# A four-layer cross-attention kernel: layer 0's head outputs joined into dense tiles, steps for the other batch moved, PSUM banks reassigned

## The chip, the cores and the metric

The kernel runs on one core of a Trainium2 chip, in one launch. The metric is the device time of one execution in microseconds (us), here the median of a few runs. The profile is one execution recorded by the hardware profiler; it has a time of its own.

## The reference

Four layers, each `x = x + attention(layernorm(x), ctx)` and then `x = x + ffn(layernorm(x))`, in fp32, with x of 4 x 256 x 256 (batch, token, width) and ctx of 4 x 512 x 128. Layer 0's attention has 16 heads of 16 columns; the last 16 context rows ("dca") have keys and values of their own, a softmax of their own, and their result is added:

```python
q = _ln((x @ Wq + bq).reshape(b, s1, H, HD), qn_w, qn_b)
...
ctx = _attn(qT, k.transpose(0, 2, 1, 3), v.transpose(0, 2, 1, 3))
...
ctx = ctx + DCA_WEIGHT * ctx_dca
return ctx @ Wo + bo
```

Layers 1 to 3 have 16 heads of 128 with 8 key and value heads, all on the same ctx. The feed-forward parts differ: F0 picks the 4 strongest of 64 small "arrows" for each token; F1 is a mixture of 8 experts, 2 for each token, plus a shared MLP; F2 picks one of two MLPs for each token; F3 sends 64 tokens of each batch through an MLP and scales the others.

## The kernel before

x stays in SBUF (`x_sb[b]`) for the whole launch. The order of the work on PE (TensorE), ACT (ScalarE), DVE (VectorE) and POOL (GpSimd) is written out by hand (`manual_schedule`): the order of the calls in the program is the order in each engine's queue, and each engine takes its queue in that order. DMAs are mostly issued by SP. The stages follow one another on the trace as layer 0's attention (0 to about 165 us), F0 with the first folding (to 244), attention 1 (to 576), F1 with the second folding (to 702), attention 2 (to 1035), F2 with the third (to 1092), attention 3 (to 1422), F3.

**PSUM.** `bank()` (L850) gives out the 8 banks. In layer 0 and F0 the tag "o" has 2 banks and all others share a ring of 6. Later "s" has 4, "mm" 2, "t" 1 and "o" 1. A step that asks for a bank waits until its last reader is done.

**Layer 0's attention** loops over 4 batches and 4 groups of 4 heads, in two halves, so 8 steps i for a batch. A step computes `scores` (L1314, with the exponential on ACT), the `values` (L1327) of the group before, after every second step its `quotient` (L1348), and beside these, in `ahead` and `between` (L1503, L1514), the next batch's Norm, projections, head norms (`Scale`, whose product writes `pad` on DVE, L1231) and transposes of `pad` (L1296), and the batch before's `output0` (L1362). Each head's values tile has 32 columns: 16 of ones, which yield the softmax divisor, and 16 of values. The output of `values` (po) thus holds divisors and results on alternate runs of 16 partitions. `quotient` transposes po in 32x32 blocks on DVE (L1354), takes the reciprocal (L1356), transposes that back in a broadcast (L1357), multiplies (L1359), and adds main and dca results on POOL into `oT` (L1360). `oT` therefore has four tiles of 128 partitions of which half are useless, and `wo0` is loaded (L1069) in four tiles likewise, so `output0` takes four matmuls for each chunk of 128 tokens (L1366), then adds the bias on DVE (y_sb, L1374) and to x on POOL (L1375). `project_v` (L1185) fills the values, three ACT copies for each batch.

**F0** runs `Arrows(n)` for the 8 token chunks: `vectors` (matmul paf), `routes` (selection on DVE, last product twof on POOL, L1427), `turned` (transposes puTf, L1435) and `output` (pyf, L1448).

**Folding** (L974) multiplies, for each layer 1 to 3, query by key weights (pm, L985; to m_sb on ACT, L993) and value by output weights (pn, L1001; to n_sb on DVE, L1004), one pair of heads after the other, both in tag "mm".

**Attention 1 to 3** (L1689) loops over b and 8 head pairs hp: scores ps (L1817), exponential on ACT (L1820), po (L1825), half sums of the probabilities on POOL and DVE (L1836 to L1850), the divisors of four pairs (pz, L1857; rz, L1866), and the division (L1871, L1872). `beside1` and `beside3` (L2117, L3051) put steps of the next feed-forward part for batch b-1 beside given head pairs: in layer 1 Norm, its tokens, `turned1` (transposes and a store, L2058) and `chosen` (the choice of experts, L2067); in layer 3 the Router's steps (L2878).

**F1** has `Shared` (L2146), and 23 `Block`s (L2290) of 128 gathered tokens: `weights` (the expert's index read into registers of PE and DVE, and its weights copied, L2312, L2317), `turn_in` (transposes pxg, L2306, to ACT), `rise` (pgu, L2325) and `fall` (pyr, L2341; yr on ACT, L2348). F2's `Block2` (L2592) is alike for 7 blocks.

```python
if b > 0 and i in (4, 5):
    output0(b - 1, (i - 4,))
```

## Time and profile before

| | us |
|---|---|
| median of 3 runs | 1453.56 |
| the runs | 1453.41, 1453.56, 1455.87 |
| the profiled execution | 1455.58 |
| its span, first to last instruction | 1453.9 |
| PE busy in it | 1421.4 |
| mean granted clock of PE | 0.994 of full speed |

The span is the profiled execution without the 1.7 us around it. A row of the profile names a line of the kernel, an engine, an operation, its output and inputs; "idle before" is the time in which that engine stood, and the name behind the arrow is the instruction whose end released it. "f32 128x256" is 128 partitions of 256 elements. A matmul in fp32 appears as two records. PEclk is the clock granted to PE, as a share of full speed.

### The profile page before, as it was taken

How to read it: one execution, taken by the hardware profiler on the slowest of the kernel's cores; microseconds unless marked ns; L12 is line 12 of the kernel's file. 1: busy time of each engine (PE TensorE's matmuls, PEld its weight loads, DVE VectorE, ACT ScalarE, POOL GpSimd, SP SyncE). 2: the span in 40 equal slices, each digit the busy share in tenths (PEclk: the TensorE clock that was granted, in tenths of full speed). 3: DMA queues.
4: the chain of work that ended last, by engine and by line, in shares of the span. 5: the costliest groups of instructions: out<-in, count | busy, mean ns of one | idle time of the engine just before them, and what ended most of it. 6: DMA issues, size and time to landing. Idle time of an engine off the chain costs nothing.

```text
span 1453.9 us, 20222 instructions
## 1 busy us (share of the span) xinstructions
PE 1421.4 (98%) x7421; PEld 937.0 (64%) x7421; DVE 914.0 (63%) x2004; ACT 585.9 (40%) x1124; POOL 677.1 (47%) x796
## 2 busy tenths in 40 slices
PE   9999999999999999999999999999999999999998
PEld 7665676566556666777556666655875566666656
DVE  6666773666676556543576666548755766767675
ACT  4666343433433332244543333333454433333331
POOL 2222232576655454131366665665314765456560
PEclk9999999999999999999999999999999999999999
DMA  5000220310000001164020000000331000000000
GB/s 167 2 2 2 73 72 1 79 32 0 8 1 8 1 8 32 39 203 103 30 72 2 23 1 1 8 0 8 95 124 44 19 1 1 0 1 0 0 1 32
DMA packets 49591, 47.06 MB, mean 32 GB/s; under 512 B 8169, under 2 KB 45386, under 8 KB 49484
## 3 DMA queue, kind: packets, MB, share of 16 engines
q1 hardware_dynamic: 45884, 37.56, 8.6%
q0 software_dynamic: 2496, 6.82, 1.8%
q8 instruction: 61, 1.00, 0.3%
q10 hardware_dynamic: 1104, 1.31, 0.3%
q14 instruction: 46, 0.38, 0.1%
HBM read 38.86 MB, written 6.82 MB: 31 GB/s over the span
## 4 chain that ended last, share of the span: by engine, by line
PE 88%; DVE 7%; POOL 2%; issue 1%; ACT 1%; DVEq 0%; ACTq 0%; POOLq 0%
PE ps L1817 22%; PE po L1825 21%; PE paq L1787 5%; PE pao L1787 4%; PE pbq L1787 4%; PE pbo L1787 4%; PE pgu L2325 2%; PE ps L1321 2%; PE pyf L1448 2%; PE po L1331 2%; PE paf L1398 1%; PE py L1907 1%; PE pm L985 1%; PE psh L2161 1%; PE pn L1001 1%
## 5 line engine op out<-in xcount | busy, mean ns | idle before, releaser
L1836 POOL TENSOR_TENSOR half<-pT 128x1024 f32<-128x1024 f32 x93 | 218.8, 2353 | 322.6 <-ACT pT L1820 255.2
L1817 PE MATMUL ps<-qT,cT 128*128 128x512 f32 x768 | 345.5, 592 | 0.0
L1825 PE MATMUL po<-pT,c_sb 128*128 128x512 f32 x768 | 345.3, 592 | 0.0
L1820 ACT ACTIVATE pT<-ps,mbias 128x512 f32<-128x512 f32 x384 | 263.7, 687 | 155.5 <-PE ps L1817 143.9
L1825 PEld LDWEIGHTS po<-pT,c_sb 128*128 128x128 f32 x768 | 145.8, 190 | 183.2 <-issue 183.2
L1817 PEld LDWEIGHTS ps<-qT,cT 128*128 128x128 f32 x768 | 138.9, 190 | 138.4 <-issue 137.0
L1829 ACT COPY oT<-po 128x512 f32<-128x512 f32 x96 | 56.2, 586 | 265.0 <-PE po L1825 265.0
L1872 POOL TENSOR_TENSOR oT<-oT,wide 128x512 f32<-128x512 f32 x90 | 115.5, 1304 | 27.9 <-DVE wide L1871 27.9
L1325 ACT ACTIVATE pT<-ps 128x512 f32<-128x512 f32 x128 | 66.1, 603 | 37.8 <-PE ps L1321 37.6
L1797 DVE TENSOR_TENSOR qT<-qT,paq 128x128 f32<-128x128 f32 x90 | 25.5, 283 | 85.8 <-ACT qT L1796 85.7
L1797 DVE TENSOR_TENSOR w<-w,pao 128x128 f32<-128x128 f32 x21 | 6.0, 285 | 109.4 <-ACT w L1796 109.4
L1844 DVE TENSOR_TENSOR half<-half 128x512 f32<-128x512 f32 x96 | 71.0, 740 | 2.5 <-POOL half L1836 2.2
L1846 DVE STREAM_TRANSPOSE turned<-half 128x512 f32<-128x512 f32 x96 | 68.3, 712 | 6.3
L1787 PEld LDWEIGHTS paq<-xnT_a,m_sb 128*128 128x128 f32 x360 | 57.9, 191 | 21.5 <-issue 10.6
L1787 PE MATMUL paq<-xnT_a,m_sb 128*128 128x128 f32 x360 | 71.4, 280 | 0.1
L1787 PE MATMUL paq<-xx,m_x 128*128 128x128 f32 x360 | 69.8, 276 | 0.0
L1850 DVE TENSOR_REDUCE sums<-turned 128x16 f32<-128x512 f32 x96 | 65.9, 686 | 3.4
L1787 PE MATMUL pao<-n_x,ox 128*128 128x128 f32 x336 | 65.4, 276 | 0.3 <-POOL ox L1713 0.3
L1871 DVE STREAM_TRANSPOSE wide<-rz 128x512 f32<-128x512 f32 x96 | 62.2, 686 | 0.1
L1796 ACT COPY qT<-paq 128x128 f32<-128x128 f32 x90 | 23.9, 265 | 89.9 <-PE paq L1787 89.8
L1800 DVE TENSOR_TENSOR qT<-qT,pbq 128x384 f32<-128x384 f32 x90 | 49.9, 554 | 9.4
L1787 PEld LDWEIGHTS paq<-xx,m_x 128*128 128x128 f32 x360 | 54.6, 192 | 0.0
(445 smaller groups left out, 2612.9 us busy)
## 6 DMA issues: line engine op xcount, KB each, us to landing
wo<-in_L_wo SPq DMA_DIRECT2D x12, 512.0 KB
wq<-in_L_wqT SPq DMA_DIRECT2D x11, 512.0 KB
yd<-yr SPq DMA_DIRECT2D x23, 128.0 KB
w<-in_F_w SPq DMA_DIRECT2D x4, 512.0 KB
xd<-xn_f SPq DMA_DIRECT2D x7, 256.0 KB
wk<-in_L_wkT SPq DMA_DIRECT2D x11, 128.0 KB
wv<-in_L_wvT SPq DMA_DIRECT2D x11, 128.0 KB
x_sb<-in_x SPq DMA_DIRECT2D x4, 256.0 KB
```

The lines of the kernel that those rows point to most:

```text
L1325: nc.scalar.activation(pT[kp][:, j], ps[j], AF.Exp)
L1787: nc.tensor.matmul(p[:, at, :], lhsT=lhsT, rhs=rhs, start=(k == 0 and at == 0), stop=(k == len(of) - 1 and i == which[-1]),)
L1817: nc.tensor.matmul(ps, lhsT=cT[:, b, k * P : (k + 1) * P], rhs=qT, start=True, stop=True)
L1820: nc.scalar.activation(pT[:, k, :], ps, AF.Exp, bias=mbias[:, b, k : k + 1])
L1825: nc.tensor.matmul(po, lhsT=c_sb[:, b, k, :], rhs=pT[:, k], start=(k == 0), stop=(k == NK - 1))
L1829: done["head"] = nc.scalar.copy(raw, po).ins
L1836: nc.gpsimd.tensor_tensor(half, pT[:, 0:2], pT[:, 2:4], ALU.add)
L1844: nc.vector.tensor_tensor(part, half[:, 0], half[:, 1], ALU.add)
L1846: nc.vector.transpose(turned.rearrange("p f i -> p (f i)"), part)
L1850: nc.vector.tensor_reduce(sums[b, hp // 4][:, hp % 4, :], turned, AX.X, ALU.add)
L1871: nc.vector.transpose(wide, rzs[b, hp // 4][:, hp % 4, :, None].to_broadcast([P, NB, 32]))
L1872: eng.tensor_tensor(outs[b, hp], outs[b, hp], wide.rearrange("p f i -> p (f i)"), ALU.mult)
```

## The change

It has six parts.

1. *Dense output tiles in layer 0.* Even groups of heads put their values in the upper and odd groups in the lower half of each 32 columns, so that two groups' results fill each other's gaps and are added into one `oT` tile. There are two tiles of `oT` and `wo0` where there were four, two matmuls a chunk in `output0` and in `output_bias`, `wo0` is loaded by eight DMAs of 16 partitions, the value weights are first copied by POOL into that order (`wvo`), `project_v` has six ACT copies, and `quotient` writes reciprocals into a tile that stays zero elsewhere and transposes that. POOL makes six adds a batch instead of four.
2. `output0(b-1)` goes from steps 4 and 5 to steps 6 and 7, except beside the last batch.
3. `arrows[0]`'s `turned` and `output` go ahead of the last `output0`.
4. In foldings 2 and 3, pn goes to banks "o" and "t".
5. In `beside1` the steps for the other batch come one head pair earlier; in `beside3` the Router's too, while its `gathered` and `rest` come one later.
6. In F1 the first two blocks' `weights` are called behind the calls that follow the list of indices, ahead of the loop over the blocks; `turn_in` of both block classes alternates between banks "t" and "o"; `fall` uses "mm".

```diff
-                pn = bank("mm", [P, 2, D], f"pn_{L}_{i}_{g}")
+                pn = bank("mm" if "ring" in banks else "ot"[g], [P, 2, D], f"pn_{L}_{i}_{g}")
...
+        wo0 = l0.tile([P, 2, D], F32, tag="wo0", name="wo0")
+        wo0r = t["L0_wo"].rearrange("(q o j i x) n -> o j i x q n", q=2, o=2, j=4, i=2)
+        for o in range(2):
+            for j in range(4):
+                r0 = 32 * j + HD0 * (1 - o)
+                nc.sync.dma_start(wo0[r0 : r0 + HD0], wo0r[o, j, 1])
...
+                for o, (h, _) in enumerate(halves):
+                    if k0 < NK:
+                        nc.scalar.copy(vals[b % 2][:, k0 : k0 + 2, o, :, h], pv[:, :, o])
+                    else:
+                        nc.scalar.copy(vals_d[b % 2][:, o, :, h], pv[:, 0, o])
...
-            nc.vector.reciprocal(rz, z[:, :, 0])
-            nc.vector.transpose(z, rz[:, :, None].to_broadcast([P, NB0, 32]))
+            odd = hg % 2
+            rz = rz0[odd]
+            nc.vector.reciprocal(rz[:, :, 1 - odd], z[:, :, HD0 * odd])
+            nc.vector.transpose(
+                z.rearrange("p f (i x) -> p f i x", i=2), rz[:, :, :, None].to_broadcast([P, NB0, 2, HD0])
+            )
...
-            nc.gpsimd.tensor_tensor(oT[:, hg, :], o[:, 0], o[:, 1], ALU.add)
+
+            oT = oT[:, hg // 2, :]
+            nc.gpsimd.tensor_tensor(oT, oT if odd else o[:, 1], o[:, 0], ALU.add)
+            if odd:
+                nc.gpsimd.tensor_tensor(oT, oT, o[:, 1], ALU.add)
...
-                for hg in range(4):
+                for q in range(2):
                     nc.tensor.matmul(
                         py,
-                        lhsT=oTs[b][:, hg, c * P : (c + 1) * P],
...
+        for n in range(2):
+            wv = by_head(wkv, 2 * HD0)[:, n, :, HD0:].rearrange("p (q o j) x -> p o q j x", q=2, o=2)
+            for o in range(2):
+                nc.gpsimd.tensor_copy(wvo[:, n, o].rearrange("p (q j) x -> p q j x", q=2), wv[:, o])
...
+            i0 = 4 if b == B - 1 else 6
+            if b > 0 and i in (i0, i0 + 1):
+                output0(b - 1, (i - i0,))
...
         arrows[1].routes()
+        arrows[0].turned()
+        arrows[0].output()
         output0(B - 1)
...
         if b > 0:
-            if hp == 4:
+            if hp == 3:
                 ahead1[b] = Norm(b - 1, f"f1_{b - 1}")
+            elif hp == 4:
+                ahead1[b] = ahead1[b].tokens()
             elif hp == 5:
-                ahead1[b] = ahead1[b].tokens()
+                turned1(b - 1, ahead1[b])
             elif hp == 6:
-                turned1(b - 1, ahead1[b])
-            elif hp == 7:
                 chosen(b - 1)
...
-                    pt = bank("t", [P, ND, P], f"pxg{self.j}")
+                    pt = bank("to"[self.j % 2], [P, ND, P], f"pxg{self.j}")
...
-                    py = bank("o", [P, D], f"pyr{j}")
+                    py = bank("mm", [P, D], f"pyr{j}")
...
             shared[1].add(1)
+            blocks[0].weights()
             shared.append(Shared(3))
             shared[3].up([0])
             shared[2].gate([2])
             shared[2].down(0)
             shared[3].gate([0])
+            blocks[1].weights()
...
         if b > 1:
-            if hp == 0:
+            if hp == 1:
                 routers[b - 2].gathered()
-            elif hp == 1:
+            elif hp == 2:
                 routers[b - 2].rest()
-            elif hp == 2 and b == 3:
-                picked(0)
+                if b == 3:
+                    picked(0)
```

## The prediction, made before the result was known

> **What bounds the kernel now.** First the page's busy times and its chain.

> ```profile
> PE 1421.4 (98%) x7421; PEld 937.0 (64%) x7421; DVE 914.0 (63%) x2004; ACT 585.9 (40%) x1124; POOL 677.1 (47%) x796
> PE 88%; DVE 7%; POOL 2%; issue 1%; ACT 1%; DVEq 0%; ACTq 0%; POOLq 0%
> ```

> TensorE is busy 1421.4 of 1453.9 us, so all its idle time is 32.5 us. Time can leave by fewer matmuls, by shorter waits of PE, or by less time at half clock. Second, the list of waits for PE (waiting group <- releaser: total us, how many, longest); these are the waits that the change touches.

> ```profile
> PE pz L1857 <- DVE sums L1850: 3.4, 3, 2.6
> PE pxg L2608 <- ACT xnT_f L940: 1.7, 1, 1.7
> PE py L1366 <- POOL oT L1360: 1.6, 1, 1.6
> PE pT L1296 <- DVE y_sb L1374: 1.4, 1, 1.4
> PE pn L1001 <- ACT m_sb L993: 1.4, 2, 0.7
> PE pT L1296 <- ACT pT L1325: 1.1, 1, 1.1
> PE pgu L2325 <- DVE we L2317: 0.7, 1, 0.7
> PE pyr L2341 <- ACT yr L2348: 0.6, 1, 0.6
> ```

> Third, the timeline (start, duration, engine, line) in layer 0: the second batch's pad and its wait, then the stage's end.

> ```profile
> 77.27 1.76 DVE L1231 TENSOR_TENSOR pad<-qk,hr 128x1536 f32<-128x1536 f32 x1
> 83.07 1.09 PE L1296 MATMUL pT<-ident,pad 128*128 128x128 f32 x8 [1.42 <-DVE y_sb L1374]
> 160.21 1.93 POOL L1427 TENSOR_TENSOR twof<-routef,vf 128x1024 f32<-128x1024 f32 x1 [5.64 <-DVE vf L1426]
> 160.26 1.46 PE L1366 MATMUL py<-wo,oT 128*128 128x256 f32 x6
> 162.53 0.72 POOL L1360 TENSOR_TENSOR oT<-o 128x256 f32<-128x256 f32 x1 [0.39 <-DVE nrf L1414]
> 163.30 2.43 PE L1366 MATMUL py<-wo,oT 128*128 128x256 f32 x10 [1.58 <-POOL oT L1360]
> ```

> The last oT add stands behind a 1.93 us POOL product, so PE waits in the middle of output0. The 16 records at 160.26 and 163.30 take 1.46 + 2.43 = 3.89 us for 8 matmuls (two records each): 0.48 us a matmul. Fourth, two-microsecond windows around the longest wait.

> ```profile
> core 0: us, PE busy (x) PEld busy (x) DVE busy (x) ACT busy (x) POOL busy (x), PEclk, DMA share, GB/s
> 562.00:564.00 2.00, 0.24 (x3) 0.05 (x1) 1.86 (x3) 0.27 (x1) 0.00 (x0) 1.00 0.01 4
> 566.00:568.00 2.00, 2.00 (x12) 2.00 (x11) 1.93 (x4) 0.00 (x0) 1.03 (x1) 0.50 0.00 0
> ```

> PE idles 562.24 to 564.88 while DVE works, and then runs at half clock: the wait has an echo.

> [...] L2608 stood 1.66 us at 1048.71 for ACT to read bank "t". [...] L1229 takes 0.72 us beside the POOL add to x_sb and 0.26 elsewhere.

> **The change, part by part.**

> *Dense output of layer 0.* 16 of 32 matmuls go, 16 x 0.48 = 7.7 us of PE, but parts of the stage are led by other engines. Last output0: PE is free at 160.26 and now first does turned(0), which needs the product ending at 162.14: a new wait of 1.9. Then output0 costs 2 x 0.97 = 1.9, its adds (two of 0.73) hidden behind turned and output of arrow 0. Before: 165.73 - 160.26 = 5.5; now 3.8; gain **1.6**. (Bounds: 0.5 if the adds are late as well, 3.5 without the wait.) Batch 3's stretch: output0 stays at steps 4 and 5 and PE leads there: 4 x 0.48 = **1.9**. Batch 1: from the scores at 71.49 to those at 89.06 the length is set by pad (ends 79.03), quotient and Norm on DVE, not by PE. With output0 moved to steps 6 and 7, PE reaches the transposes earlier and the y_sb and x_sb adds no longer stand before pad; pad ends about 77.9, DVE's remaining order lets these scores start about 87.5: **1.6**, bounds 0 (DVE takes it back) and 1.9. Batch 2 the same, less sharply: **1.4**, bounds 0 and 1.9. output_bias loses two matmuls (0.9), but the wait for pad behind it (the 1.1 us of pT L1296 <- ACT pT) ends at 47.07 whatever PE does: 0. bias_columns' two small matmuls: 0.25.
> Cost: project_v's copies at the start sit ahead of ACT's power for the first pad. Before 2 x 0.583 + 0.38 = 1.55; now four of 256 elements at 0.38 and two of 128 at 0.27 (L1796's row) = 2.05, so **-0.5**, bounds 0 and -1. For batches 2 and 3 ACT has slack.
> Costed at nothing: four weight copies on POOL (about 1.1 us, POOL idle from 8 to 16 us; unhidden 1.1). Eight loads of 16 partitions for one on SP's queue (about 0.4 us of issue each, estimated from neighbouring issues, so 3 us later for what is queued behind; wo0 is first read near 40, the mask at 57, wa at 145). Two more 0.73 us adds a batch on POOL, busy 37 of the first 150 us. The second transpose reads 16-wide repeats of a 32-column tile; no row has that pattern. The broadcast form L1871 takes 0.686 against 0.712 for the plain one, so I take 0.71; lower bound the same, upper bound unknown and priced as a rival.
> Sum: 1.6 + 1.9 + 1.6 + 1.4 + 0.25 - 0.5 = **6.2**, bounds 2.5 and 8.5.

> *Steps one head pair earlier, attention 1.* The 2.6 us are due to chosen (DVE 558.6 to 561.8), which stood behind pl and ahead of the last pair's sums. Moved to pair 6 it waits for its pl there (DVE idles in front of pl anyway, with about 2 us to give before pair 7's divisor); the sums then end near 561, PE reaches pz about 561.5. Gain **2.6**, and with it the half clock at 565: the second products cost 4.36 instead of 2.56 us, of which only 0.7 counts, since DVE and POOL then bound the last division: **0.7**. Norm now lands on pair 3: 1.35 us of DVE against 3.2 of slack there. turned1's DMA of 256 KB goes out a pair earlier on SP, past nothing that is needed before 590. *Attention 3:* gathered waited 2 x 0.3 on rz and now lies behind it, and the last pz loses 0.3: **0.9**. spread's and places' DVE work has the same slack; no DMA is among them. Bounds of both: 1 and 6; sum **4.2**.

> *F1.* The first blocks' weights: 0.74 of pgu <- we goes; PE's register load now waits, if at all, in front of shared[3], for an index ready at 602 where PE comes at 603 or later; 0 if it holds, up to -1 if late, and the down and gate matmuls are queued behind it. Banks "t" and "o" in turn remove 0.46 on L2306; 0.2 of both lost: **1.0**. pyr's 0.56 with two banks "mm": **0.5**. Folding 2: pn 0.7 and pm 0.5, in banks of their own; late next is the copy of n_sb: **1.2**. Sum **2.7**, bounds 1 and 4. *F2.* pxg 1.66 behind xnT_f and 0.46 more go with the second bank: 2.1; folding 3's pn 0.7, of which 0.5: sum **2.6**, bounds 1 and 3.5.

> **Total** 6.2 + 4.2 + 2.7 + 2.6 = **15.7**. The profiled execution took 1455.58 (span 1453.9, 1.7 around it): 1455.58 - 15.7 = 1439.9. It stands 2.02 above the median of 1453.56; against that, 1437.9, said as **1438.0**. Not in the sum: where half-clock windows fall. Those near 565, 600 and 777 can each come or go; the one at 600 stretches the pysh group from 2.6 to 5.3 us.

> **Rivals.**
> *Half of layer 0 and of the moved steps comes back.* DVE's chain pad, quotient, qT bounds batches 1 and 2, so both gains go (-3.0); the last output gives 0.5 (-1.1), the values' copies cost 0.5 more, and moved steps return 2: 15.7 - 6.6 = 9.1, time **1444.5**. For it: DVE's waits are short in 71 to 89. Against it: y_sb leaves exactly there.
> *Windows fall well.* With the wait at 562 gone and less waiting near 596 and 777, two windows vanish, about 2 each: **1434**.
> *Layer 0 is wholly led by DVE and the waits turn up one step later:* what stays is bias_columns 0.25, pyr 0.5 and the last output's lower bound 0.5, less the copies' 0.5: 0.75, **1452.8**, within 0.2% (2.9 us, about what a measurement of this kernel can tell from no change).
> *Slower.* One mechanism: the second transpose of quotient in layer 0 is slow in its new repeating pattern. DVE waited 24.1 us over 12 quotients for po, 2.0 each, which hides a first part. It decides the sign from 0.71 + 2.0 + 15.7/16 = 3.7 us a transpose. At six times its time, 4.25, it costs 16 x (3.54 - 2.0) = 24.6: 1453.56 - 15.7 + 24.6 = **1462.5**. Against it, the broadcast row at 0.686.

> **How the numbers follow.** Forecast 0.52 (own range 1434 to 1443), half back 0.24, windows 0.15, same 0.05, slower 0.04. The range 1431.5 to 1446 takes in the first three with their window scatter; 0.09 and the edges are left out. Faster 0.52 + 0.24 + 0.15 = 0.91, same 0.05, slower 0.04.

> **What would show it.** PE busy down about 8 in the stretch to 166; py L1366 no longer waiting on oT, a wait of puTf on twof near 160 of some 1.9 in its place; pz's total wait under 1; L2608 and pn L1001 gone from the list, pxg in F1 under 0.3; no half clock at 565. L1357 still at 0.71. Wrong it would be if puTf's wait is 3 or more, pT L1296 keeps its 1.4, or chosen's DVE work shows up as a wait of pair 6 or 7.

## The result and the profile after

The changed kernel takes 1438.83 us (median of 4 runs, 1437.80 to 1440.28) beside 1453.63 before; the ratio is 0.9895 with a 95% interval of 0.9878 to 0.9913. The forecast was 1438.0. The profiled execution took 1440.28 with a span of 1438.5, beside 1455.58 and 1453.9: 15.3 us less where the sum said 15.7. That agreement is in part luck: two groups of terms fell short, three gave more than was said, and one of these three gave it only because a stretch at half clock was absent. Most of what follows is on these.

The page's busy times and the chain of work that ended last, after. This chain was followed back over a quarter of the span only, so it says little here.

```profile
PE 1411.2 (98%) x7381; PEld 929.8 (65%) x7381; DVE 895.9 (62%) x2005; ACT 585.9 (41%) x1136; POOL 684.3 (48%) x816
PE 24%; DVE 1%; POOL 0%; DMA 0%; issue 0%
```

PE has 40 records less (two for each of 20 matmuls) and is busy 10.2 us less. The list of waits for PE, after (total us, how many, longest):

```profile
PE puTf L1461 <- POOL twof L1453: 3.0, 2, 1.8
PE pxn_a L937 <- DVE n_sb L1004: 3.0, 2, 2.1
PE pT L1315 <- DVE pad L1244: 2.7, 3, 1.5
PE pwr L3120 <- DVE n_sb L1004: 0.8, 1, 0.8
PE pn L1001 <- DVE n_sb L1004: 0.7, 1, 0.7
PE pz L1893 <- DVE sums L1886: 0.3, 1, 0.3
PE pgu L2361 <- ACT xgT L2344: 0.2, 1, 0.2
PE pb L2672 <- ACT xgT L2649: 0.2, 1, 0.2
```

Of the eight waits shown of before, five are gone, the one for pz is down to 0.3 us, and two in layer 0 go on under another releaser: pT's 1.4 us behind y_sb is 0.6 for pad, and pT's 1.1 us near 47 is the 1.5 us for pad. The first three lines are new or longer. The one for twof was forecast (1.9). The 2.1 us of pxn_a, with 0.8 of pwr, was not; neither was the 1.5 us for pad. The timeline in layer 0, after, at the places shown before:

```profile
77.69 1.76 DVE L1244 TENSOR_TENSOR pad<-qk,hr 128x1536 f32<-128x1536 f32 x1
79.60 1.50 PE L1315 MATMUL pT<-ident,pad 128*128 128x128 f32 x12 [0.59 <-DVE pad L1244]
158.02 1.93 POOL L1453 TENSOR_TENSOR twof<-routef,vf 128x1024 f32<-128x1024 f32 x1 [5.63 <-DVE vf L1452]
160.00 1.09 PE L1461 MATMUL puTf<-ident,twof 128*128 128x128 f32 x8 [1.75 <-POOL twof L1453]
165.25 1.89 PE L1392 MATMUL py<-wo,oT 128*128 128x256 f32 x8
```

The last output0 runs in one piece of 1.89 us; PE's idle time has moved ahead of it. The windows after, at the end of attention 1 and early in layer 0 (columns as in the prediction's windows):

```profile
558.00:560.00 2.00, 2.00 (x20) 2.00 (x19) 1.24 (x4) 0.27 (x1) 0.00 (x0) 1.00 0.00 0
48.00:50.00 2.00, 2.00 (x16) 1.66 (x20) 1.90 (x4) 1.10 (x3) 0.00 (x0) 0.72 0.00 0
50.00:52.00 2.00, 2.00 (x20) 0.73 (x16) 1.90 (x7) 0.68 (x1) 1.49 (x3) 0.50 0.00 0
```

The half clock at the end of attention 1 is gone. A stretch of it stands near 49 us and another at 28.4. Before, there was none at either place:

```profile
48.00:50.00 2.00, 2.00 (x31) 1.24 (x33) 1.92 (x5) 1.53 (x3) 0.47 (x1) 1.00 0.01 4
```

**By stage.** The boundaries are first records on PE's timeline: the first scores, the first pm, each attention's first pq, F1's first psh, attention 2's last pz (its second record), F3's first ph; F3 ends with PE's last record. PE's idle time and the us at half clock are beside each length.

| stage | before: us, idle, half | after: us, idle, half | gain | forecast |
|---|---|---|---|---|
| start | 24.52, 1.89, 0 | 23.99, 2.01, 0 | 0.53 | -0.5 |
| layer 0, to the first pm | 163.99, 7.37, 0 | 160.92, 7.50, 6.82 | 3.07 | 6.7 |
| rest of F0, folding 1 | 55.42, 2.81, 0 | 55.41, 2.80, 0 | 0.01 | 0 |
| attention 1 | 332.47, 2.64, 3.41 | 329.28, 0.78, 0 | 3.19 | 3.3 |
| F1, folding 2 | 125.48, 4.78, 6.83 | 121.36, 2.13, 6.83 | 4.12 | 2.7 |
| attention 2, to the last pz | 320.72, 1.47, 3.41 | 319.14, 1.61, 0 | 1.58 | 0 |
| F2, folding 3 | 69.30, 2.80, 0 | 69.29, 3.19, 0 | 0.01 | 2.6 |
| attention 3 | 334.41, 1.60, 0 | 331.84, 0.40, 0 | 2.57 | 0.9 |
| F3 | 21.49, 1.04, 0 | 21.48, 1.04, 0 | 0.01 | 0 |

Layer 0 and F2 fell short by 2.6 us each (start and layer 0 together); F1, attention 2 and attention 3 brought 4.7 more.

### The profile page after: what moved, and what is told of

It reads as the page before. It is cut to its first block, busy times and chain, and to the rows that moved or that the text cites. A ratio compares the mean times of both kernels' runs of the same rounds, so it can differ in the third digit from the quotient of the medians.

```text
span 1438.5 us, 20192 instructions
## 1 busy us (share of the span) xinstructions
PE 1411.2 (98%) x7381; PEld 929.8 (65%) x7381; DVE 895.9 (62%) x2005; ACT 585.9 (41%) x1136; POOL 684.3 (48%) x816
## 3 DMA queue, kind: packets, MB, share of 16 engines
q0 software_dynamic: 2496, 6.82, 1.9%
HBM read 38.60 MB, written 6.82 MB: 32 GB/s over the span
```

## The experiments

Each group of runs had the kernel before beside it on the same chip (medians of 1455.65 for 1 to 4, 1455.12 for 5 to 8 and 1455.31 us for 9 to 12). Where no half-clock stretch comes or goes, stage lengths repeat to some 0.1 us from one profile to the next, those of F1, attention 2 and F2 to some 0.5 to 0.7, so the stages decide more than the medians do. The start took 23.99 to 25.53 us in the twelve traces with the new layer 0. It follows the moment at which the trace first shows PE at full clock, 4.51 us in the shortest and 7.71 in the longest.

**1. The changed kernel once more.** No edit.

> The changed kernel once more, unaltered. Theory A (where half-clock stretches fall is chance): its median is again 1438 to 1440, the profile shows half-clock stretches at other places than 28.6, 49.1 and 591.8, and layer 0 up to the first folding product is shorter by about 1.7 us for each of the two that is missing there (184.9 before, then 183.2 or 181.5). Theory B [...]: the stretches near 28 and 49 are there again and the first folding product starts at 184.9 within 0.3.

Measured: 1439.65 us, ratio 0.9892 (0.9877 to 0.9907). Layer 0 took 159.28 with one stretch, at 48.6; the one at 28.4 was missing. So a stretch costs 160.92 - 159.28 = 1.64 us here, and of the two one is chance and one may be caused: each theory holds for one. (Run 10 has both again.) Every other stage repeated within 0.1 us but the start (25.51) and F2 (68.83).

**2. Layer 0's parts alone**, and **3. everything but them.** The edits are the hunks of the diff themselves.

> The kernel before with only layer 0's parts of the change (dense tiles, output0 moved, arrow 0's turned and output moved). The forecast's sum says 6.2 us off, 1447.4. Theory A: between 3 and 6.5 off, depending on how many half-clock stretches of about 1.7 us fall into layer 0; everything after 244 us like the kernel before, with the 2.6 us wait for pz at the end of attention 1 back. Theory B: 3.6 off or less, with two stretches near 28 and 49 us.

> The changed kernel with layer 0 as before. The parts outside layer 0 together: the forecast's terms say 9.5 us off the kernel before, so 1444.1. By the stages of the changed kernel's trace attention 1 gives 3.2, F1 4.1, attention 2 1.6 (a half-clock stretch that may come back), F2 0, attention 3 2.6: 11.5 with the stretch gone and 9.9 with it, so 1442.1 to 1443.7. F2 with its folding stays at 69.3 and PE waits about 2.1 us for n_sb ahead of pxn_a.

Measured: layer 0 alone 1448.70, ratio 0.9959 (0.9946 to 0.9973); the rest alone 1445.00, ratio 0.9925 (0.9911 to 0.9938). In the profile of the first, layer 0 takes 159.16 with one stretch, at 46.5: 4.83 gained, so 6.5 without the stretch. The second has attention 1 at 329.27, F1 at 121.61, F2 at 68.89, attention 3 at 331.85 and attention 2 at 320.62 with its stretch back. The parts add up: 0.41% and 0.75% make 1.16%, beside 1.08% for the run of 1 and 1.05% for the first measurement. What attention 2 gave is the stretch and nothing of the change. By the stages theory A of the first expectation and the sums of the second hold. By the medians both are past them: 6.95 us off where theory A said 6.5 at most (1.66 of it, in the profiled run, is attention 2 without its stretch), and 10.65 off where the sums said 9.9 with the stretch.

**4. Folding 3's second products in another bank**, and **5. back in mm.** The first added line is 4's, the second 5's.

```diff
-                pn = bank("mm" if "ring" in banks else "ot"[g], [P, 2, D], f"pn_{L}_{i}_{g}")
+                pn = bank("mm" if "ring" in banks else "s" if L == 3 else "ot"[g], [P, 2, D], f"pn_{L}_{i}_{g}")
...
+                pn = bank("mm" if "ring" in banks or L == 3 else "ot"[g], [P, 2, D], f"pn_{L}_{i}_{g}")
```

> The changed kernel with the second products of the third folding in the four banks s in place of o and t. Theory: pxn_a waited 2.1 us and pwr 0.8 us because bank t was held by a product whose copy stood behind the next layer's norm on DVE; with t free, F2 with its folding takes about 66.5 in place of 69.3, and the time falls by 2.5 to 2.9 us against the changed kernel (about 1436). Rival: what is late next is the norm itself (its tokens end at 1072.3, pxn_a could start at 1071.7), so 2 us or more of the wait stay and the time falls by less than 1 us.

> The changed kernel with the third folding's second products back in mm (that part of the change undone for layer 3 alone). Theory (bank t held by a copy behind the norm cost what the part gained): the wait for pxn_a goes, the 0.7 us of pn for m_sb comes back, F2 with its folding takes 67 to 67.6 in place of 68.8 to 69.3, and the kernel is 1 to 2 us faster than the changed one. Rival (the part is worth its forecast 0.5 and the wait comes from F2's other edits): F2 takes 69.3 or more and the kernel is 0.5 us slower.

The timeline of DVE and of PE at the end of folding 3, changed kernel:

```profile
1071.50 0.80 DVE L925 TENSOR_SCALAR xn_a<-x_sb,mv_a,rstd_a 128x256 f32<-128x256 f32 x2 [0.85 <-POOL rstd_a L920]
1072.22 0.68 DVE L1004 COPY n_sb<-pn 128x512 f32<-128x512 f32 x1
1072.82 0.41 DVE L2719 TENSOR_TENSOR x_sb<-x_sb,yg 128x256 f32<-128x256 f32 x1
1073.16 0.68 DVE L1004 COPY n_sb<-pn 128x512 f32<-128x512 f32 x1
```

```profile
1070.79 1.02 PE L1001 MATMUL pn<-wo,wv 128*128 128x512 f32 x2
1073.89 0.66 PE L937 MATMUL pxn_a<-ident,xn_a 128*128 128x128 f32 x4 [2.08 <-DVE n_sb L1004]
```

The norm's tokens stand on DVE ahead of two copies of n_sb, and wait there 0.85 us for POOL. The product of the first had ended at 1070.06, ahead of that wait; its copy still came behind the norm, at 1072.22. The second copy empties bank "t", ends at 1073.84, and only then can pxn_a, which also lives in "t", start, though its own input was ready at 1072.3. With bank "s", the same place:

```profile
1070.11 1.02 PE L1001 MATMUL pn<-wo,wv 128*128 128x512 f32 x2
1071.36 0.76 PE L937 MATMUL pxn_a<-ident,xn_a 128*128 128x128 f32 x4 [0.22 <-DVE xn_a L925]
```

Measured: F2 66.11 with "s" and 67.38 with "mm", beside 68.83 in run 1; medians 1437.38 (ratio 0.9872, 0.9857 to 0.9887) and 1438.44 (0.9887, 0.9872 to 0.9902). Both theories hold by the stage. The medians are 2.3 and 1.2 us below run 1's, and the intervals of the ratios overlap with its own. By the stage the new banks for these products cost 1.45 us against no change at all there.

**6. Arrow 3's vectors ahead of arrow 0's turned.**

```diff
         arrows[1].routes()
+        arrows[3] = Arrows(3)
+        arrows[3].vectors()
         arrows[0].turned()
...
-                if n + 3 < B * NC:
+                if 0 < n < B * NC - 3:
```

> The changed kernel with the vectors of arrow 3 called ahead of arrow 0's turned, so that PE has 3.4 us of work while POOL makes the product twof. Theory: the new wait of puTf on twof (1.75 us) is what is left of the last output's gain; it goes, and the start of the first folding product comes 1.5 to 1.8 us earlier. Rival: ACT must read arrow 3's vectors before it copies the turned tiles (4 reads of 0.5 us), so pyf waits in its place and less than 0.7 us is won.

Measured: layer 0 157.30, still with its one stretch, beside 159.28: 1.98 less, and PE's idle time in it 5.76 in place of 7.53. The wait of 1.75 is gone and none took its place, so the rival falls. Median 1437.42, ratio 0.9886 (0.9870 to 0.9902): not told apart from the changed kernel by time.

**7. output0 at steps 4 and 5 for all batches**, and **8. arrow 0 behind the last output0 again.**

```diff
-            i0 = 4 if b == B - 1 else 6
+            i0 = 4
...
-        arrows[0].turned()
-        arrows[0].output()
         output0(B - 1)
...
-            if n:
-                arrows[n].turned()
+            arrows[n].turned()
...
-                if n:
-                    arrows[n].output()
+                arrows[n].output()
```

> The changed kernel with output0 at steps 4 and 5 for all batches. By the forecast's working the move is what lets pad end earlier in batches 1 and 2: layer 0 grows by 1.5 to 2.5 us. Rival (DVE's chain from pad to qT sets these batches whichever step output0 stands in): within 0.5 us, since the two y_sb adds of 0.42 us each only change places.

> The changed kernel with arrow 0's turned and output back behind the last output0. Theory: PE then stands in the last output0 for two POOL adds that end about 161.9 in place of 1.75 us for twof; the wait is about 3.2 us, so up to the first folding product 1.3 to 1.7 us are lost. Rival: the later start of arrow 0 only moves work, and less than 0.5 us is lost.

The waits of 7, then of 8, on the two places:

```profile
PE pT L1315 <- DVE y_sb L1400: 3.5, 2, 2.3
```

```profile
PE py L1392 <- POOL oT L1386: 3.3, 1, 3.3
```

Measured: 1443.63 (0.9922, 0.9908 to 0.9935) and 1442.13 (0.9914, 0.9901 to 0.9928). In 7 layer 0 takes 162.20 with 6.83 us of half clock: without the added stretch 1.3 us more than in run 1, with it 2.9. The added stretch begins at 116.7, behind a wait of 1.30; the wait of 2.25, which ends at 84.2, brought none. In 8 it takes 163.72 with 10.24 us: 1.53 more idle, as expected, and 6.83 us more of half clock from 161.2 on, while PE still stood in the wait of 3.3, so 4.4 us in all. Both rivals fall. In 8 the long wait was paid for twice, and that part of the loss was not expected.

**9. score_bound behind pad.** Only the place of 1.2 us of DVE work changes.

```diff
-                elif i == 3:
-                    score_bound()
                 elif i == 4:
                     output_bias()
+                elif i == 7:
+                    score_bound()
```

> The changed kernel with score_bound called at step 7 in place of step 3 of batch 0, so that its 1.2 us of DVE come behind pad and not ahead of it. Theory (PE's 1.5 us wait for pad at 46.4, which output_bias's two missing matmuls only made longer, brings the half-clock stretch near 48.5): pad ends 1.2 us earlier, the wait shrinks to about 0.3, the stretch is gone, and layer 0 takes 156.5 to 158 in place of 159.3. Rival (the stretch comes with the clock's own rhythm): it is there again within 2 us of 48.5, and layer 0 gains 1.2 at most.

Measured: 1439.28 (0.9892, 0.9877 to 0.9908), no faster. In the profile the wait for pad near 46 is down to 0.66 and the stretch near 48 is gone; layer 0 takes 158.12. This run took 1437.53; the other three took 1439.2 to 1439.9, and whether they had a stretch is not known. The windows of this run at the place:

```profile
46.00:48.00 2.00, 2.00 (x28) 1.55 (x27) 1.90 (x4) 2.00 (x4) 0.00 (x0) 1.00 0.00 0
48.00:50.00 2.00, 1.45 (x24) 0.72 (x16) 1.90 (x7) 0.83 (x3) 1.56 (x3) 1.00 0.00 0
```

PE waits instead:

```profile
PE pT L1315 <- DVE pad L1244: 1.8, 3, 0.7
PE pT L1315 <- DVE qT L1327: 1.1, 1, 1.1
```

The idle time did not shrink (7.85 beside 7.53): DVE's chain of pad, quotient, norm and qT sets this part, and the wait only moved one transpose further on. The theory holds for the stretch, in this profile and in that of run 12, and fails for the wait. The stretch began between 46.5 and 48.9 in all ten traces that have layer 0's change without this edit, and in neither of the two with the old layer 0. It is not the clock's rhythm alone: in run 2 it begins 0.3 us before the end of the wait for pad. In the trace of before the clock's pieces, carried back from its later stretches (last section), have a boundary 0.4 us before the end of that wait, which was then 1.13 us, and no stretch began.

**10. The other batch's steps back at their old head pairs.** The edit undoes the hunks of beside1 and beside3.

> The changed kernel with the steps of beside1 and beside3 back at their old head pairs. Theory: attention 1 takes 331.9 to 332.5 again in place of 329.3 (the 2.6 us wait for pz is back, with a half-clock stretch or not) and attention 3 takes 334.4 in place of 331.8; 5.2 to 5.8 us are lost, 1444.5 to 1445.5. Rival (the gain of attention 3 came from elsewhere, since its listed waits add up to about 1.2): attention 3 takes 333 or less.

```profile
PE pz L1893 <- DVE sums L1886: 3.4, 3, 2.6
PE pxg L3000 <- DVE rz L1902: 0.6, 2, 0.3
```

Measured: attention 1 332.43, attention 3 334.42; 1444.04, ratio 0.9924 (0.9910 to 0.9938). The lines of before are back to the digit. The rival falls: all of attention 3's 2.57 us is due to these steps.

**11. F1's and F2's blocks as before.** Banks "t" for turn_in and "o" for fall, and both first weights inside the loop.

> The changed kernel with the blocks of F1 and F2 as before (their banks and the first two blocks' weights undone). Theory: F1 with its folding loses the 0.74 for the weights, 0.46 less 0.24 for bank t and 0.56 for pyr: 1.5 us, 122.8; F2 loses 1.66 + 0.46 less 0.24: about 1.9 us; 3.4 in all. Rival: F2's waits come later only because its folding's wait for n_sb ends when DVE's norm does, and that moves along with it: F2 loses 1 us or less.

Measured: F1 123.14 (1.80 more than run 1), F2 70.59 (1.76 more); 1442.66, ratio 0.9912 (0.9897 to 0.9927). Theory within 0.3 us in both; the rival falls.

**12. The edits of 4, 6 and 9 together.**

> The changed kernel with the three edits that the traces point to: the third folding's second products in bank s, arrow 3's vectors ahead of arrow 0's turned, score_bound behind pad. If they add up: 2.7 + 1.8 + 1.6 to 2.8 off the changed kernel, 1432 to 1434 beside 1439.7 for the changed one and 1455.5 for the one before. Rival: the saved waits only shift where half-clock stretches fall, and one or two of 1.6 us come back: 1435 to 1437.

Measured: 1433.59 (1431.30 to 1436.87), ratio 0.9849 (0.9836 to 0.9863), which lies clear of the changed kernel's 0.9892 in run 1. It beats both kernels. Its profile was of the slowest of the five runs, 1436.87, and shows F2 at 66.05 and layer 0 at 157.50, with no stretch near 48, but one at 129.8 and one at 764.6 in attention 2, which others of these runs may not have had.

## Why the prediction was right, and where it was wrong

**Layer 0 (6.2 forecast, 3.6 in the first profile, 4.9 in run 2).** Without stretches the gain from the first scores on would be 6.4 to 6.5, an estimate that takes the 1.64 of run 1 for each, so the mechanism was right in the main. The parts, from the starts of the score groups in run 1: batch 1 1.27 for 1.6, batch 2 1.22 for 1.4, batch 3 1.21 for 1.9, the last output 1.42 for 1.6, and batch 0, which has the stretch near 49 in it, lost 0.41 where 0.25 was to be gained. In batch 3 the term 0.48 us a matmul was mis-sized: a chunk went from 1.83 to 1.01 us (starts 136.04 to 137.87 before, 134.94 to 135.95 in run 1), 0.41 for each matmul removed. It also got a new wait of 0.23 us for xn_f, and pays 0.43 in all there. Why batches 1 and 2, priced by VectorE's order, are short was not separated. The values' copies were to cost 0.5 at the start. Between traces that first show full clock at the same moment, the start is 0.12 to 0.13 us longer than with the old layer 0 (an estimate between neighbouring traces).

The step that failed is "the wait for pad behind it ... ends at 47.07 whatever PE does: 0". Counted from the first scores, pad ends only 0.4 us earlier in run 1, while PE comes earlier and stands 1.5 us for it in place of 1.1. In ten traces of ten half clock began between 0.3 us before and 1.0 us after that wait's end. I costed this at nothing. Run 9's profile, without the stretch, has layer 0 1.16 us shorter. That the two matmuls missing from output_bias make the wait longer is read from the order of the work; no run puts them back alone.

**Attention 1 (3.3, measured 3.19).** Right by both terms' sum. The echo of 0.7 was too much: run 2 has the 2.6 us wait without any stretch and takes 332.15, only 0.32 less than with one.

**F1 (2.7, measured 4.12).** The blocks gave 1.80 for 1.5 (run 11). Folding 2, from its first pm to attention 2's first pq, went from 20.15 to 18.07, 2.08 for 1.2: besides the listed waits, stops between its products that were too short for the list are gone. The other 0.24 is within what F1 differs by from profile to profile.

**Attention 2 (0, measured 1.58).** A half-clock stretch at 777 that the changed kernel did not have:

```profile
778.00:780.00 2.00, 2.00 (x12) 2.00 (x11) 0.99 (x3) 0.27 (x1) 1.92 (x3) 0.50 0.00 0
```

Of the 14 traces three have it, at the end of the first batch (777.3 before, 770.2 in run 3, 764.6 in run 12). Two of them are the only two with the old layer 0, so chance alone would be a weak account; the last section shows where in the clock's pieces each of the traces met this place. The prediction left it out of the sum, and luck gave it.

**F2 (2.6, measured 0.01).** "folding 3's pn 0.7, of which 0.5" failed. The blocks' 2.1 came as 1.76. Folding 3, from its first pm to attention 3's first pq, went from 23.51 us to 25.09 in run 1, and took 22.35 with the products in "s". The new banks for pn lost what these brought: I looked at who waited for the old bank, not at who else uses the new ones, nor at what stands ahead of the copy that frees them.

**Attention 3 (0.9, measured 2.57).** The mechanism held (run 10), the size did not. From start to start of PE's records the two stops of pxg behind pz cost 0.96 us and not the 0.6 listed, the last stop of pz 0.64 in place of the 0.47 listed, of which I took 0.3. Another 0.6 among the paq products and 0.2 in pxg lay in stops too short for the list.

**Banks, half clock and the rivals.** In the changed kernel's profile pxn_a waited 2.08 us for bank "t", whose reader stood on DVE behind the norm; in run 4, with the products in other banks, it waited 0.22 us. Before, half clock followed a wait of 2.64 us; in the changed kernel's profile it also followed a shorter one: the 1.48 us for pad ended at 47.95, and half clock began at 48.88. The slow transpose of the "slower" rival does not exist: L1377's 16 take 711 ns each, beside 712 for the plain one (L1846, in the profile of before).

## What to carry to other kernels

Before a tile gets another PSUM bank, list who shares that bank and what stands ahead of its reader in the reader's queue: 2.1 us of wait hung on a copy behind a norm. Where PE leads, a wait was in some cases here followed by a half-clock stretch, of some 1.6 us (1.64 by run 1) on top of its own length, and in others not: of the 38 waits of PE of 1.4 us or more between 20 and 1405 us in the 14 traces, 14 had a stretch begin in them or within 3.4 us behind them, ten of these at the one place near 48. Look for work to put there (run 6), and compare stages with the stretches counted. A sum that comes out right proves none of its terms.

## What the runs showed of the hardware that was not expected

Attention 2 shows what comes of that. Its stretch began 75.4, 75.5 and 75.7 us after its first pq in the three traces that have it. In the other eleven the grid's point nearest to these was at 74.0 to 75.0 (nine), 75.8 and 76.2, and no stretch began. The work there is the same in all; the grid point at 75.4 to 75.7 is what the three have in common.

PE's idle time can be added up for each piece of the grid, here between 25 and 1405 us of all 14 traces. All four pieces with 2.07 us or more were followed by half clock (2.64 in the trace of before), and none of the 19 with 1.50 to 1.87 was (1.55 and 1.66 in the trace of before, 1.75 in the changed kernel's first). The wait for pxn_a of 2.0 to 2.1 us was followed by a stretch in one trace of nine, the one in which it lay in a single piece.

Below that, idle time alone does not tell: the ten waits for pad of 1.5 us near 48 were all followed by it. It also came with little idle time ahead of it: at 28.4 in the changed kernel's profile, and in run 10, after these windows:

```profile
24.00:26.00 2.00, 1.62 (x17) 1.02 (x16) 2.00 (x5) 0.96 (x3) 1.86 (x8) 1.00 0.63 175
26.00:28.00 2.00, 1.95 (x20) 1.40 (x20) 0.72 (x3) 2.00 (x6) 2.00 (x9) 1.00 0.00 0
28.00:30.00 2.00, 2.00 (x7) 1.49 (x6) 0.00 (x0) 1.99 (x5) 0.85 (x4) 0.60 0.00 0
```

PE idles 0.43 us in these 4.4 us, in which it does the scores of 16 rows and transposes. What brought half clock there was not shown.
